# Twenty output products put off to the end of a graph-attention layer, and their bias as one bf16 product

## The chip, the cores and the metric

The kernel runs on one core of a Trainium2 chip. The metric is the device time of one execution in microseconds, as the median of several runs. The profile is one execution, in which every instruction of TensorE (PE), VectorE (DVE), ScalarE (ACT), GpSimd (POOL) and the DMA queues is recorded with its start and duration.

## The reference

Sixteen batches of 1024 nodes with 512 features pass through eight-head attention over one graph that all batches share, an output projection, a residual addition and a layer norm without scale:

```python
q = (x @ Wq + bq).reshape(b, n, H, HD)          # b = 16, n = 1024, H = 8, HD = 64, all float32
k = (x @ Wk + bk).reshape(b, n, H, HD)
v = (x @ Wv + bv).reshape(b, n, H, HD)
scores = jnp.einsum('bqhd,bkhd->bhqk', q, k) / jnp.sqrt(jnp.float32(HD))
scores = scores + (1.0 - adj)[None, None, :, :] * -1000000000.0
attn = jax.nn.softmax(scores, axis=-1)
out = jnp.einsum('bhqk,bkhd->bqhd', attn, v).reshape(b, n, d)
y = out @ Wo + bo
return _layernorm(x + y, axis=-1)
```

The graph is sparse: a node has few neighbours, and the number varies from node to node.

## The kernel before

**Tiles and blocks.** The nodes are ranked by their number of neighbours once, and each batch is worked in eight tiles of 128 ranked nodes. The attention of a tile is a list of blocks: for block i, every one of the 128 nodes takes its i-th neighbour, whose key and value row is gathered from DRAM by an indirect DMA on POOL (`gather`, line 961, 128 rows of 4 KB into `kvg`). VectorE multiplies queries with keys (`products`, line 982) and sums by head (`scores`, line 986); ScalarE takes the exponentials (line 996) and weighs the values (line 1006), VectorE adds them up (line 1022). The few nodes with more neighbours get extra blocks, which TensorE adds with a selection matrix (`sum`, lines 1031 and 1032). A batch has 34 blocks, all batches together 544.

**Front products.** Ahead of the attention of a batch come its transposes of x (`pxT`), its query products (`pq`, line 619) and key and value products, done as a seven-product scheme of block combinations (`x`, `pp`, `z`, line 743, with the elementwise combinations on VectorE). They run about two batches ahead and go to DRAM as `q_rows` and `kv_rows`.

**Output.** `normalise` and `turn` divide by the sum of the weights and transpose the result (`poT`), and ScalarE copies it to `oT`. `finish` then issues four products with Wo (`po`, line 619) for the tile, adds residual and bias, and normalises: line 844 adds the residual and line 845 the bias with the row sum, ScalarE squares and applies the norm (lines 852 and 866), and POOL scatters the rows to the output (line 870). Once the front products are over and blocks are left, the bias is added by TensorE instead: a fifth f32 product of a column of ones with the bias (line 917, `biased`), so that VectorE has one operation per tile there, not two.

**Put off.** Ten tiles, numbers 102 to 111 of 128, are not finished in turn. Their `oT` goes to DRAM (`spill`), and after the front products it is brought back (`reload`, line 815, into the free tiles e, w and g) together with the residual. For tiles from 102 on the residual is kept in DRAM in ranked order as well (`residual`, stored at line 593 when x has been transposed, loaded at line 809), so that it comes back by a plain DMA on SyncE and not by a gather on POOL (line 797).

**Order.** The order of all instructions is fixed when the program is built. A loop runs over steps n from -39 to the end; step n does the early parts of blocks n+4, n+3 and so on and the last part of block n, and then hands TensorE work from two lists, `finishing` before `fronts`, as long as a credit lasts. The credit grows in each step by a share, which in the middle is what the front products and the output products of a batch need:

```python
share = (max(0.0, left - goal) + NT * NPAIR * PRODUCT + NS * SUM) / NBT
```

From batch 13 on the share spreads the rest of the front products up to step 498; after that it is `LAST_SHARE`. Each engine and each DMA queue takes its instructions strictly in this order. Work meant for a later step is put in by `later` (in the same step ahead of the block's last part) and `later_last`.

Of the kernel before, what the change touches and what calls it, by code (L numbers as in the profile page):

```python
# [10 lines left out]
F32 = mybir.dt.float32  # L11
BF16 = mybir.dt.bfloat16
I32 = mybir.dt.int32
AF = mybir.ActivationFunctionType
OP = mybir.AluOpType
# [16 lines left out]
KG_BUFS, Q_BUFS, QT_BUFS, PV_BUFS, Y_BUFS = 8, 5, 3, 5, 6  # L32
# [3 lines left out]

LAZY = 2

SPILL = range(102, 112)

AHEAD_LAST = 11

# [1 line left out]
EARLY = 13  # L44

FIRST = 11
# [9 lines left out]
PRODUCT = 0.86  # L56
SUM = 0.87
TRANSPOSE = 0.44
LEAD_SHARE = 3.3
START_SHARE = 2.0  # L60
LAST_SHARE = 3.0

P = 128

# [102 lines left out]
def kernel(  # L167
# [36 lines left out]
    nc = tc.nc  # L204
    B, N, D = x.shape
    HD = D // HEADS
    NPAIR = D // P
# [35 lines left out]
    with ExitStack() as main:  # L243
# [24 lines left out]
        before = one.tile([P, P], F32, name="before")  # L268
        bq_bc = one.tile([P, D], F32, name="bq_bc")
        bk_norm = one.tile([P, 1], F32, name="bk_norm")  # L270

        B11, B21, B22, T1, T2, T3, T4 = (
            work.tile([P, 2, D], F32, tag=name, name=name, bufs=1) for name in ("b11", "b21", "b22", "t1", "t2", "t3", "t4")
# [24 lines left out]
        order_views = dram_disjoint_views(order, NT)  # L298
        out_views = dram_disjoint_views(out, B * NT)
        x_rows = x.rearrange("b n d -> (b n) d")  # L300
        spill = [dram.tile([P, D], F32, name=f"spill_{i}") for i in range(len(SPILL))]
        residual = [dram.tile([P, D], F32, name=f"residual_{i}") for i in range(B * NT - SPILL[0])]
        zeros = work.tile([P, D + HEADS], F32, tag="pv0", name="zeros", bufs=3)
        nc.gpsimd.memset(zeros, 0.0)
        bias_rows = work.tile([2 * NPAIR, D + HEADS], F32, tag="pv0", name="bias_rows", bufs=3)[:, 0:P]
# [58 lines left out]
            nc.vector.tensor_tensor(bo_bc, pb, bo_bc, op=OP.add)  # L364

        now, plan, rest, urgent, known, waiting, combined = [0], {}, {}, [], [], [], []

        def later(k, fn):  # L370
            plan.setdefault(now[0] + k, []).append(fn)
# [209 lines left out]
        def transpose_x(b, t):  # L581
            def pe():
                xs = X.pop((b, t))
                p = fill_psum(f"pxT_{b}_{t}")
                for c in range(NPAIR):
                    nc.tensor.transpose(p[:, ts(c, P)], xs[:, ts(c, P)], ident)  # L586

                def out():
                    XT[b, t] = work.tile([P, D], F32, tag="xT", name=f"xT_{b}_{t}", bufs=4)
                    nc.scalar.copy(XT[b, t], p)  # L590
                    n = b * NT + t + 3
                    if b * NT + t >= SPILL[0]:
                        nc.sync.dma_start(residual[b * NT + t - SPILL[0]], xs)
                        later(2, lambda: load_x(n // NT, n % NT))
                    else:
                        load_x(n // NT, n % NT)
                    if t % 2 and (b, t) != (0, 1):
                        later(1, combine)

                def combine():  # L600
                    s = [work.tile([P, HD2], F32, tag=f"s{i}", name=f"s{i}_{b}_{t}", bufs=1 + i // 4) for i in (1, 2, 3, 4)]
                    x0, x1 = XT[b, t - 1], XT[b, t]
                    nc.vector.tensor_tensor(s[0], x1[:, 0:HD2], x1[:, HD2:D], op=OP.add)
                    nc.vector.tensor_tensor(s[2], x0[:, 0:HD2], x1[:, 0:HD2], op=OP.subtract)
                    nc.vector.tensor_tensor(s[1], s[0], x0[:, 0:HD2], op=OP.subtract)  # L605
                    nc.vector.tensor_tensor(s[3], x0[:, HD2:D], s[1], op=OP.subtract)
                    SX[b, t // 2] = s

                later(1, out)

            return [(TRANSPOSE, pe, lambda: (b, t) in X)]
# [179 lines left out]
            units += unit("z", s(4), B22, False, out_v0, "v1")  # L791
            return units

        loaded, half = {}, []

        def gather_x(y, b, t):
            nc.gpsimd.indirect_dma_start(  # L797
# [4 lines left out]
        def load_y(b, t, k=None):  # L802
            if k is None:
                Y[b, t] = work.tile([P, D], F32, tag="y", name=f"y_{b}_{t}", bufs=Y_BUFS)
            else:
                Y[b, t] = work.tile([P, 2, D], F32, tag=f"t{k % 4 + 1}", name=f"y_{b}_{t}", bufs=1)[:, 0, :]
            loaded[b, t] = now[0]
            if b * NT + t >= SPILL[0]:
                nc.sync.dma_start(Y[b, t], residual[b * NT + t - SPILL[0]])
            else:  # L810
                gather_x(Y[b, t], b, t)

        def reload(b, t, k):
            OT[b, t] = work.tile([P, D], F32, tag="ewg"[k % 3], name=f"oTs_{b}_{t}", bufs=1)
            nc.sync.dma_start(OT[b, t], spill[b * NT + t - SPILL[0]])
            load_y(b, t, k)
            later(2, lambda: done.append((b, t)))

        def finish(b, t):
# [9 lines left out]
            def out(p):  # L829
# [4 lines left out]
                if single:  # L834
                    st = small.tile([P, 5], F32, name="stats", bufs=6)
                else:

                    second = bool(half)
                    if not second:
                        half.append([small.tile([P, 2, 5], F32, name="stats_2", bufs=3)])  # L840
                    st2 = half[0][0]
                    st = st2[:, int(second), :]
                if fronts_then:
# [71 lines left out]
            if biased:  # L915
                def bias():
                    nc.tensor.matmul(
                        PS[f"po_{b}_{t}"], ident[:, 0:1].to_broadcast([P, P]), bo_bc, start=False, stop=False
                    )

                units.insert(2, (PRODUCT, bias, None))
            return units


# [136 lines left out]
        def turn(b, t, o):  # L1061
            def transpose():
                p = fill_psum(f"poT_{b}_{t}")
                for c in range(NPAIR):
                    nc.tensor.transpose(p[:, ts(c, P)], o[:, ts(c, P)], ident)  # L1065

                def out():
                    OT[b, t] = work.tile([P, D], F32, tag="oT", name=f"oT_{b}_{t}", bufs=LAZY + 2)
                    nc.scalar.copy(OT[b, t], p)
                    if b * NT + t in SPILL:  # L1070
                        later(1, lambda: nc.sync.dma_start(spill[b * NT + t - SPILL[0]], OT.pop((b, t))))
                        spilled.append((b, t))
                    else:
                        later(1, lambda: done.append((b, t)))

                later(1, out)

            later(1, lambda: urgent.append(transpose))
            if not fronts:
                coming.append((b, t))  # L1080
# [71 lines left out]
        prep.setdefault(CHECKS_AT, []).append(checks())  # L1152
        preps = [loads(), ranks()]
        prep.setdefault((B - 1) * NBT, []).append(guard())
        with tc.manual_schedule():

            fronts += transpose_x(0, 0) + transpose_x(0, 1)
# [11 lines left out]
            while n < total or plan or rest or urgent or done or finishing or spilled or not guarded:  # L1169
                now[0] = n  # L1170
                if n < 0:
                    share = START_SHARE if n > FRONT_BY else LEAD_SHARE if n > -LEAD_IN else TRANSPOSE * 1.5
                elif n >= SPILL[0] // NT * NBT + NBT:

                    share = sum(u[0] for u in fronts) / max(fronts_end - n, 1) + NS * SUM / NBT if fronts else LAST_SHARE
                elif n % NBT == 0:

                    left = sum(u[0] for u in fronts)
                    ahead = EARLY + FIRST * (1 - max(0, n // NBT - 1) / (SPILL[0] // NT))
                    goal = fronts_time - (n // NBT + 2 + ahead / NBT) * batch_time  # L1180
                    share = (max(0.0, left - goal) + NT * NPAIR * PRODUCT + NS * SUM) / NBT
                if 0 <= n + 3 < total:
                    exponentials(n + 3)
                if 0 <= n + 4 < total:
# [25 lines left out]
                    if tile_done not in loaded and sum(b * NT + t not in SPILL for b, t in Y) < 5:  # L1210
                        load_y(*tile_done)
                coming[:] = [t for t in coming if t not in loaded]
                if spilled and not fronts and n > last_reload + 2 and sum(b * NT + t in SPILL for b, t in Y) < 3:
                    reload(*spilled.pop(0), reloads)
                    reloads, last_reload = reloads + 1, n
                first_unit = True
                while credit > 0 or urgent:
                    if urgent and not (first_unit and fronts):
                        urgent.pop(0)()
                        continue  # L1220
                    if (
                        not finishing and len(done) > (LAZY if fronts else 0) and n > loaded.get(done[0], n) + 1
                        and n > last_finish + 1 and not total - 2 <= n < total
                    ):
                        finishing = finish(*done.pop(0))
                        last_finish = n
                    units = finishing or fronts
                    if not units:
                        if urgent:
                            urgent.pop(0)()  # L1230
                            continue
                        break
                    cost, fn, ready = units[0]
                    if ready and not ready():
                        if urgent:
                            urgent.pop(0)()
                            continue
                        break
                    del units[0]
                    fn()  # L1240
                    credit -= cost
                    first_unit = False
# [40 lines left out]
```

## Time and profile before

| | us |
|---|---|
| median of 3 runs | 1944.96 |
| lowest and highest | 1942.09, 1947.64 |
| the profiled execution's own time | 1947.77 |
| its span, first to last instruction | 1946.0 |

The profile counts busy time as the union of an engine's instructions. An f32 product is two instructions (the output products are 1024 instructions), and successive ones overlap, so the mean duration of a row is longer than what one costs in a series; the distance between starts is that. "DMA share" is the mean busy share of the core's 16 DMA engines.

### The profile page before, as it was taken

What the parts mean: (1) busy time and instruction counts of PE and PEld (TensorE: products, weight loads), DVE (VectorE), ACT (ScalarE), POOL (GpSimd) and SP (SyncE); (2) the same over time, 40 slices, a digit from 0 to 9 for tenths busy, and PEclk for the clock granted to TensorE, in tenths of its full rate; (3) what the DMA queues carried; (4) which work ended last, traced back from release to release, by engine and by line L of the source; (5) the groups of instructions that cost most, each with busy time, mean ns of one, the idle gap of its engine ahead of it and who ended that gap; (6) DMA issues with size and microseconds to landing.
All of it is one profiled execution on the core that took longest, in us unless ns stands there. A gap on an engine that the chain in (4) does not pass through costs nothing.

```text
span 1946.0 us, 25024 instructions
## 1 busy us (share of the span) xinstructions
PE 1872.7 (96%) x5259; PEld 905.5 (47%) x5259; DVE 1730.4 (89%) x3496; ACT 1550.5 (80%) x6072; POOL 1380.3 (71%) x1283
## 2 busy tenths in 40 slices
PE   8989999899999999999999999999999999889896
PEld 3434454444544454444545445454544444344443
DVE  6888889899998999989999989999998998989894
ACT  3638779778888888888888878888888798879694
POOL 1336667878787677877887777777777777766684
PEclk9999999999999999999999999999999999999998
DMA  7357788888889788887888888888888989998994
GB/s 271 121 177 244 249 275 271 289 271 285 290 276 315 252 296 274 272 309 256 300 280 301 275 279 304 288 296 269 296 295 291 317 284 350 320 328 267 349 302 146
DMA packets 183104, 541.40 MB, mean 278 GB/s; under 512 B 30783, under 2 KB 30795, under 8 KB 182942
## 3 DMA queue, kind: packets, MB, share of 16 engines
q0 software_dynamic: 134864, 451.79, 69.5%
q1 hardware_dynamic: 45184, 82.41, 11.8%
q10 hardware_dynamic: 2894, 5.52, 0.9%
q8 instruction: 44, 0.72, 0.1%
q14 instruction: 118, 0.97, 0.1%
HBM read 423.93 MB, written 140.37 MB: 290 GB/s over the span
## 4 chain that ended last, share of the span: by engine, by line
PE 73%; DVE 10%; DMA 5%; issue 3%; ACT 2%; POOL 1%; SPq 0%; POOLq 0%; DVEq 0%; ACTq 0%
PE po L619 18%; PE pq L619 16%; PE pp L743 13%; PE z L743 9%; PE x L743 9%; DMA kvg<-kv_rows,key_row 2%; DVE qk L982 2%; PE poT L1065 2%; PE pxT L586 2%; DVE s L986 2%; PE sum L1032 2%; PE sum L1031 1%; ACT pv L1006 1%; DVE pv L1022 1%; PE pm L688 1%
## 5 line engine op out<-in xcount | busy, mean ns | idle before, releaser
L1006 ACT ACTIVATE pv<-kvg,pv 128x64 f32<-128x64 f32 x3544 | 892.6, 339 | 0.0
L961 POOL DMA_INDIRECT kvg<-kv_rows,key_row x544 | 621.3, 1142 | 233.2 <-issue 85.9
L619 PE MATMUL po<-wo,oT 128*128 128x512 f32 x944 | 437.4, 596 | 2.0 <-DVE y L844 1.1
L619 PE MATMUL pq<-wq,xT 128*128 128x512 f32 x904 | 425.9, 600 | 0.9 <-DVE g L762 0.7
L986 DVE TENSOR_REDUCE s<-qk 128x8 f32<-128x512 f32 x544 | 369.8, 680 | 8.1 <-ACT y L866 0.5
L982 DVE TENSOR_TENSOR qk<-qt,kvg 128x512 f32<-128x512 f32 x448 | 306.2, 683 | 35.8 <-DMA kvg<-kv_rows,key_row 29.9
L619 PEld LDWEIGHTS po<-wo,oT 128*128 128x128 f32 x944 | 176.9, 191 | 199.2 <-issue 185.5
L619 PEld LDWEIGHTS pq<-wq,xT 128*128 128x128 f32 x904 | 169.2, 192 | 196.3 <-issue 179.0
L743 PE MATMUL pp<-t,s 128*128 128x512 f32 x504 | 237.1, 593 | 0.5 <-DVE s L605 0.5
L743 PE MATMUL x<-b,xT 128*128 128x512 f32 x504 | 237.0, 592 | 0.0
L1022 DVE TENSOR_TENSOR pv<-pv,pv 128x520 f32<-128x520 f32 x336 | 232.9, 693 | 1.5 <-ACT pv L1006 1.5
L996 ACT ACTIVATE pv<-s,absent 128x8 f32<-128x8 f32 x448 | 130.4, 294 | 81.5 <-DVE s L986 75.4
L797 POOL DMA_INDIRECT x<-in_x_dram,asked_row x120 | 133.7, 1114 | 76.7 <-PE pxT L586 46.1
L870 POOL DMA_INDIRECT out_dram<-y,asked_row x128 | 144.9, 1132 | 36.5 <-issue 21.4
L665 POOL DMA_INDIRECT kv_rows<-kv,asked_row x120 | 138.9, 1158 | 35.1 <-issue 20.9
L629 ACT ACTIVATE sq_k<-kv 128x128 f32<-128x128 f32 x512 | 150.9, 300 | 6.3 <-DVE kv L766 6.3
L743 PEld LDWEIGHTS x<-b,xT 128*128 128x128 f32 x504 | 94.7, 190 | 113.6 <-issue 109.2
L743 PEld LDWEIGHTS pp<-t,s 128*128 128x128 f32 x504 | 94.5, 190 | 110.7 <-issue 101.6
L931 POOL DMA_INDIRECT qg<-q_rows,query_row x96 | 108.1, 1126 | 34.2 <-issue 23.8
L797 POOL DMA_INDIRECT y<-in_x_dram,asked_row x102 | 108.8, 1066 | 32.3 <-issue 30.2
L743 PE MATMUL z<-b,s 128*128 128x512 f32 x252 | 120.7, 602 | 5.1 <-DVE kv L771 4.9
L743 PE MATMUL z<-t,s 128*128 128x512 f32 x252 | 120.6, 601 | 0.0
(200 smaller groups left out, 2666.8 us busy)
## 6 DMA issues: line engine op xcount, KB each, us to landing
q_rows<-q SPq DMA_DIRECT2D x113, 256.0 KB
qt<-q_rows SPq DMA_DIRECT2D x105, 256.0 KB
kvg<-kv_rows,key_row POOLq DMA_INDIRECT x544, 5.8
residual<-x SPq DMA_DIRECT2D x26, 256.0 KB
y<-residual SPq DMA_DIRECT2D x26, 256.0 KB
adj<-in_adj_dram POOLq DMA_DIRECT2D x8, 512.0 KB, 12.7
kv_rows<-kv SPq DMA_DIRECT2D x8, 512.0 KB
spill<-oT SPq DMA_DIRECT2D x10, 256.0 KB
```

The source lines that it names most:

```text
L619: nc.tensor.matmul(p, lhs(c), w[:, c, :], start=(c == 0), stop=(c == NPAIR - 1))
L629: nc.scalar.activation(sq, s[:, ts(h, P)], AF.Square, scale=scale, accum_out=sums[:, h:h + 1])
L665: later(2, lambda: nc.gpsimd.indirect_dma_start(out=kv_views[b % ROWS][tt[i]], out_offset=bass.IndirectOffsetOnAxis(ap=asked_row[:, tt[i]: ...
L743: nc.tensor.matmul(R[bank], l[:, ts(c, P)], right[:, c, :], start=(first and c == 0), stop=(c == 1), skip_group_check=True,)
L797: nc.gpsimd.indirect_dma_start(out=y, out_offset=None, in_=x_rows, in_offset=bass.IndirectOffsetOnAxis(ap=asked_row[:, t:t + 1], axis=0), ...
L870: nc.gpsimd.indirect_dma_start(out=out_rows[b, t], out_offset=bass.IndirectOffsetOnAxis(ap=asked_row[:, t:t + 1], axis=0), in_=y, in_offse ...
L961: nc.gpsimd.indirect_dma_start(out=KG[n], out_offset=None, in_=kv_rows[b % ROWS], in_offset=bass.IndirectOffsetOnAxis(ap=key_row[:, g:g + ...
L982: nc.vector.tensor_tensor(QK[n], q, KG[n][:, 0:D], op=OP.mult)
L986: nc.vector.tensor_reduce(S[n], QK.pop(n).rearrange("p (h d) -> p h d", d=HD), axis=AX.X, op=OP.add)
L996: nc.scalar.activation(PV[n][:, D:], S.pop(n), AF.Exp, bias=bias)
L1006: nc.scalar.activation(pv[:, ts(h, HD)], v[:, ds(D + h * HD, HD)], AF.Copy, scale=pv[:, D + h:D + h + 1])
L1022: nc.vector.tensor_tensor(PV[b, t], PV[b, t], pv, op=OP.add)
```

## The change

The tiles put off become twenty: every fourth tile from number 36 to 96 (the first and fifth tile of a batch, from the fifth tile of batch 4 to the first of batch 12), and 102 to 105. Tiles 106 to 111 are finished in turn again. The residual is stored in DRAM for all of these and for all tiles from 102 on. The share of a batch counts only the output products that stay in it, and the reference point of the schedule's lead (`LATE`) stays at batch 12. After the front products a reload comes in every second step instead of every third, up to seven reloaded residuals may be held instead of three (two to a double tile, of seven tile names instead of four), and a tile may be finished in every step instead of every second.

The bias product of these tiles is one bf16 product: `bias_pieces` splits the bias once into three bf16 values, the rounded bias, the rounded rest and the rest of the rest, in rows 0, 32 and 64 of `bo_3`, and `three` is a column with ones in those rows.

```diff
-SPILL = range(102, 112)
+SPILL = (*range(36, 100, 4), *range(102, 106))
+STORED = {*SPILL, *range(102, 128)}
+LATE = 12
...
-LAST_SHARE = 3.0
+LAST_SHARE = 3.4
+BIAS = 0.22
...
+        def bias_pieces():
+
+            r = work.tile([P, D], F32, tag="y", name="bo_rest", bufs=Y_BUFS)
+            nc.vector.tensor_copy(bo_3, bo_bc)
+            nc.vector.tensor_tensor(r, bo_bc, bo_3, op=OP.subtract)
+            yield
+            nc.vector.tensor_copy(bo_3[32:33, :], r[32:33, :])
+            nc.vector.tensor_copy(bo_3[64:65, :], r[64:65, :])
+            nc.vector.tensor_tensor(r[64:65, :], r[64:65, :], bo_3[64:65, :], op=OP.subtract)
+            nc.vector.tensor_copy(bo_3[64:65, :], r[64:65, :])
+            yield
+            st = small.tile([P, 1], F32, name="two", bufs=1)
+            nc.vector.tensor_tensor(st, ident[:, 0:1], ident[:, 32:33], op=OP.add)
+            nc.vector.tensor_tensor(three, st, ident[:, 64:65], op=OP.add)
...
-                    if b * NT + t >= SPILL[0]:
-                        nc.sync.dma_start(residual[b * NT + t - SPILL[0]], xs)
+                    if b * NT + t in STORED:
+                        nc.sync.dma_start(residual[b * NT + t], xs)
                         later(2, lambda: load_x(n // NT, n % NT))
...
-                Y[b, t] = work.tile([P, 2, D], F32, tag=f"t{k % 4 + 1}", name=f"y_{b}_{t}", bufs=1)[:, 0, :]
+                if k % 2 == 0:
+                    tag = ("t1", "t2", "t3", "t4", "b11", "b21", "b22")[k // 2 % 7]
+                    wide.append(work.tile([P, 2, D], F32, tag=tag, name=f"y_{b}_{t}", bufs=1))
+                Y[b, t] = wide[-1][:, k % 2, :]
...
-                        half.append([small.tile([P, 2, 5], F32, name="stats_2", bufs=3)])
+                        half.append([small.tile([P, 2, 5], F32, name="stats_2", bufs=5)])
...
-                        PS[f"po_{b}_{t}"], ident[:, 0:1].to_broadcast([P, P]), bo_bc, start=False, stop=False
+                        PS[f"po_{b}_{t}"], three.to_broadcast([P, P]), bo_3, start=False, stop=False
...
-                units.insert(2, (PRODUCT, bias, None))
+                units.insert(2, (BIAS, bias, None))
...
+        prep.setdefault(NBT, []).append(bias_pieces())
...
-                elif n >= SPILL[0] // NT * NBT + NBT:
+                elif n >= (LATE + 1) * NBT:
...
-                    share = (max(0.0, left - goal) + NT * NPAIR * PRODUCT + NS * SUM) / NBT
+                    kept = sum(i not in SPILL for i in range(n // NBT * NT, n // NBT * NT + NT))
+                    share = (max(0.0, left - goal) + kept * NPAIR * PRODUCT + NS * SUM) / NBT
...
-                if spilled and not fronts and n > last_reload + 2 and sum(b * NT + t in SPILL for b, t in Y) < 3:
+                if spilled and not fronts and n > last_reload + 1 and sum(b * NT + t in SPILL for b, t in Y) < 7:
...
-                        and n > last_finish + 1 and not total - 2 <= n < total
+                        and n > last_finish + bool(fronts) and not total - 2 <= n < total
```

More of the change, by code (lines that the diff above doesn't have):

```diff
@@ L270 @@
         bk_norm = one.tile([P, 1], F32, name="bk_norm")
+        bo_3 = one.tile([P, D], BF16, name="bo_3")
+        three = one.tile([P, 1], BF16, name="three")
         B11, B21, B22, T1, T2, T3, T4 = (
@@ L300 @@
         x_rows = x.rearrange("b n d -> (b n) d")
-        spill = [dram.tile([P, D], F32, name=f"spill_{i}") for i in range(len(SPILL))]
-        residual = [dram.tile([P, D], F32, name=f"residual_{i}") for i in range(B * NT - SPILL[0])]
+        spill = {i: dram.tile([P, D], F32, name=f"spill_{i}") for i in SPILL}
+        residual = {i: dram.tile([P, D], F32, name=f"residual_{i}") for i in sorted(STORED)}
         zeros = work.tile([P, D + HEADS], F32, tag="pv0", name="zeros", bufs=3)
@@ L792, in pair @@
             return units
-        loaded, half = {}, []
+        loaded, half, wide = {}, [], []
         def gather_x(y, b, t):
@@ L805, in load_y @@
             else:
-                Y[b, t] = work.tile([P, 2, D], F32, tag=f"t{k % 4 + 1}", name=f"y_{b}_{t}", bufs=1)[:, 0, :]
+                if k % 2 == 0:
+                    tag = ("t1", "t2", "t3", "t4", "b11", "b21", "b22")[k // 2 % 7]
+                    wide.append(work.tile([P, 2, D], F32, tag=tag, name=f"y_{b}_{t}", bufs=1))
+                Y[b, t] = wide[-1][:, k % 2, :]
             loaded[b, t] = now[0]
-            if b * NT + t >= SPILL[0]:
-                nc.sync.dma_start(Y[b, t], residual[b * NT + t - SPILL[0]])
+            if b * NT + t in STORED:
+                nc.sync.dma_start(Y[b, t], residual[b * NT + t])
             else:
@@ L814, in reload @@
             OT[b, t] = work.tile([P, D], F32, tag="ewg"[k % 3], name=f"oTs_{b}_{t}", bufs=1)
-            nc.sync.dma_start(OT[b, t], spill[b * NT + t - SPILL[0]])
+            nc.sync.dma_start(OT[b, t], spill[b * NT + t])
             load_y(b, t, k)
@@ L1070, in out @@
                     if b * NT + t in SPILL:
-                        later(1, lambda: nc.sync.dma_start(spill[b * NT + t - SPILL[0]], OT.pop((b, t))))
+                        later(1, lambda: nc.sync.dma_start(spill[b * NT + t], OT.pop((b, t))))
                         spilled.append((b, t))
@@ L1178 @@
                     left = sum(u[0] for u in fronts)
-                    ahead = EARLY + FIRST * (1 - max(0, n // NBT - 1) / (SPILL[0] // NT))
+                    ahead = EARLY + FIRST * (1 - max(0, n // NBT - 1) / LATE)
                     goal = fronts_time - (n // NBT + 2 + ahead / NBT) * batch_time
-                    share = (max(0.0, left - goal) + NT * NPAIR * PRODUCT + NS * SUM) / NBT
+                    kept = sum(i not in SPILL for i in range(n // NBT * NT, n // NBT * NT + NT))
+                    share = (max(0.0, left - goal) + kept * NPAIR * PRODUCT + NS * SUM) / NBT
                 if 0 <= n + 3 < total:
```

## The prediction

> **What bounds the kernel now.** I read the page first (busy shares, the 40 slices, the chain), then the groups, then the busy time by stage, and last the waits and the timeline of the tail.
>
> ```profile
> PE 1872.7 (96%) x5259; PEld 905.5 (47%) x5259; DVE 1730.4 (89%) x3496; ACT 1550.5 (80%) x6072; POOL 1380.3 (71%) x1283
> ...
> PE   8989999899999999999999999999999999889896
> ...
> DMA  7357788888889788887888888888888989998994
> ...
> PE 73%; DVE 10%; DMA 5%; issue 3%; ACT 2%; POOL 1%; SPq 0%; POOLq 0%; DVEq 0%; ACTq 0%
> ```
>
> TensorE carries 73% of the chain and is at nine tenths in nearly every slice until the last seven. There its digit falls to 8 and 6 while DMA rises to 9. So there are stages with different limits, and the change moves work from one to another. A step of the schedule multiplies block n+4 by its keys, so the times of line 982 on VectorE date the steps: step 136 (batch 4) is at 612.5, 442 (batch 13) at 1630.0, 474 at 1722.4, 498 (the front products end) at 1795.6, 538 at 1908.0. Busy time by stage:
>
> ```profile
> core 0: us, PE busy (x) PEld busy (x) DVE busy (x) ACT busy (x) POOL busy (x), PEclk, DMA share, GB/s
> 612.50:1630.00 1017.50, 1005.95 (x2860) 488.68 (x2859) 933.70 (x1852) 855.58 (x3398) 780.91 (x726) 1.00 0.86 289
> 1630.00:1722.40 92.40, 81.96 (x236) 39.67 (x234) 86.40 (x159) 81.94 (x349) 67.76 (x58) 0.98 0.95 333
> 1722.40:1795.60 73.20, 69.68 (x188) 34.02 (x189) 69.75 (x136) 62.38 (x249) 43.91 (x40) 0.95 0.82 282
> 1795.60:1908.00 112.40, 103.26 (x273) 47.85 (x272) 99.00 (x236) 92.97 (x336) 85.24 (x77) 0.97 0.92 322
> 1908.00:1946.00 38.00, 21.52 (x59) 10.83 (x57) 13.46 (x47) 11.94 (x25) 13.10 (x13) 0.85 0.29 104
> 320.60:386.80 66.20, 60.10 (x177) 30.76 (x176) 56.56 (x114) 56.41 (x230) 53.57 (x49) 0.98 0.86 285
> ```
>
> In batches 4 to 12 TensorE is busy 99% and VectorE 92%. Busy overlaps in a pipelined engine, so I price TensorE by starts. The timeline:
>
> ```profile
> 1784.45 3.60 PE L619 MATMUL po<-wo,oT 128*128 128x512 f32 x8
> 1787.88 1.88 PE L743 MATMUL pp<-t,s 128*128 128x512 f32 x4
> ...
> 1801.22 1.02 PE L917 MATMUL po<-bo_bc,ident 128*128 128x512 f32 x2
> 1802.07 1.88 PE L619 MATMUL po<-wo,oT 128*128 128x512 f32 x4
> ```
>
> Four f32 products take 1787.88 - 1784.45 = 3.43 us, 0.858 each; a bias product is two such instructions, 0.85. Multiplied with the instructions as built, steps 136 to 441 hold 999.6 us of TensorE work in 1017.5 us of time: TensorE is the limit there, with 2% lost. Steps 442 to 497 hold 144.4 in 165.6, and 498 to the end 115.1 in 150.4: the tail has TensorE time to spare, 21 and 35 us.
>
> **The change part by part.** All counts are from the two built orders.
>
> *Batches 4 to 12.* Sixteen tiles leave: output products fall from 284 to 220, 64 x 0.858 = 54.9 us. The smaller share also lets eight front products and eight transposes slip past step 441, 7.8 us. TensorE work: 999.6 to 936.9. At the old 2% loss that gives 954 us. VectorE loses for each tile these two (busy, mean ns of one, then idle before), and two small ones:
>
> ```profile
> L845 DVE SCALAR_TENSOR_TENSOR y<-bo_bc,y 128x512 f32<-128x512 f32 x105 | 72.8, 694 | 3.6
> L844 DVE TENSOR_TENSOR y<-po,y 128x512 f32<-128x512 f32 x105 | 71.7, 683 | 11.7 <-PE po L619 11.7
> ```
>
> and one of the waits (total us, times, longest) is
>
> ```profile
> DVE qk L982 <- DMA kvg<-kv_rows,key_row: 33.6, 27, 4.3
> ```
>
> Back to back in the chain, such an operation costs 0.61, so a tile is about 0.61 + 0.69 + 2 x 0.15 = 1.6 us, 16 of them 25.6: VectorE 933.7 to 908. VectorE cannot be full: at 1630 to 1722.4, where ten tiles were put off already and TensorE had room, it was busy 86.40 / 92.40 = 0.935. At that share 908 takes 971 us. So TensorE's limit is 954, VectorE's 971. Part of VectorE's idle time today is waiting for TensorE (11.7 us in the row above), which shrinks, and what is late next is the key gather (33.6 us over the span). I take 966, a gain of 51; ends -64 and, at the share of the last window above (56.56 / 66.20 = 0.854, so 1063 us), +46, which is where the slower rival comes from.
>
> *Batches 13 and 14 to the end of the front products.* Tiles 106 to 111 are finished in place: 24 more output products (20.6 us) plus the slipped front work, 144.4 to 172.7. The share formula of this stretch does not count output products, so the fronts crowd into the last steps: 34.8 us of TensorE work in steps 490 to 497 against 28.8. Steps 442 to 473 were VectorE's (92.4 us) and get 5 more of its work: 97. Steps 474 to 497 hold 88.5 us of TensorE work against 70.5 in 73.2: at 0.98, 90. Together 187 against 165.6: +22 (ends +16, +28).
>
> *The tail.* Output products go from 92 to 132 (+34.4 us). The bias: 22 f32 products, 18.9 us, become 32 bf16 ones. No row shows a bf16 product. The nearest is the f32 one: two instructions of 0.43. One bf16 instruction can cost from 0.21 (half of one f32 instruction) to 0.43; the Trainium skill, "TensorE: Matmul & The Clock Gate", section "Back-to-back issue gap", gives 215.7 ns for 512 columns, and an exact half of the row agrees, so I take 0.22, 7 us; at 0.43 it is 7 more. TensorE work 115.1 to 137.4, of it in steps 498 to 537 from 98.1 to 121.8. That part took 112.4; 121.8 at a share of 0.95 is 128: +16. Ten more reloads, ten more residual loads and ten more stores are 30 x 0.262 = 7.9 MB on top of 322 GB/s x 112.4 us = 36.2 MB. Here a rule speaks against the change: the skill's "DMA: Bandwidth & Descriptors", section "Specifications", puts a core's HBM limit at about 358 GB/s, which makes 44.1 MB an estimate of 123 us. By the row, 322 at a share of 0.92 is 350 at full, 126 us, and 1820 to 1840 moved 392, 112 us. I use 126, so DMA and TensorE come to about the same, and two equal limits cost a little: +17 (ends +10, +30). The end after 1908, a chain of one last tile, keeps its 38.
>
> *The clock.* The same TensorE page, Part 1, says an idle window of about 3.4 us halves the clock for one; here the granted clock is 1.00 in the full middle, and 0.98 and 0.95 in the two looser rows after it, 0.86 between 1722.4 and 1746.1. The rule speaks against loosening the middle. By the row, 0.98 of 966 would cost 19 us if TensorE were critical at each dip; as the dips come where it idles, I count three of them at 1.7, 5 us, inside my 966. By the rule alone, with every stall a dip, the gain of 51 would be 32.
>
> *Costed at nothing.* The split of the bias (six operations of 512 columns and two small ones, 4 us of VectorE in batch 1) lies beside TensorE, which has no idle time from 274.6 to 350: +1, 4 without that cover. SyncE gets 27 more stores in the middle (16 spills, 11 residuals; 7.1 MB on 289 x 1.0175 = 294, while 16 gathers of 0.262 leave POOL, so +1% net); they queue behind q stores on which SyncE waits anyway. The store that now reads x lets the gather of x three tiles on start two steps later on POOL; a pair of transposes comes every eight steps, which hides it. If not, key gathers behind it on POOL wait about 2 us each time, 27 times at most. The larger limits on buffers (seven residuals, five statistics) and a finish in every step instead of every second only permit; what they let in is priced in the tail.
>
> **Sum.** -51 + 1 + 22 + 17 = -11. The profiled execution took 1947.77 (span 1946.0); it becomes 1936.8. Its time is 2.8 above the median of the runs, 1944.96, so I predict 1934.
>
> **The rivals.** *TensorE limits throughout (-30).* The middle at 954 and a tail that packs: -64 + 1 + 20 + 13 = -30, 1915. For it: 222.8 us of batches 9 and 10 with TensorE never idle; VectorE held 44.91 of 45.50 us at 1630 to 1675.5. Against: both engines then need over 95%.
>
> *The middle becomes VectorE's and the gathers' (slower).* The mechanism: with TensorE lighter, each late key gather stops the multiply on line 982, and everything behind it on VectorE, and no TensorE backlog covers that. The price: VectorE at a share of 0.91 makes the middle 998, a gain of 19 against 40 given back: +21, 1966. It decides at 908 / (1017.5 - 40) = 0.929; above, the change gains. For it: 320.6 to 386.8, with a TensorE load as light as the new one, ran no faster than the rest (3.31 us per step). Against: 0.935 at 1630 to 1722.4 with DMA at 0.95.
>
> *Reloads come late.* A reload stands two steps before its product instead of three, in SyncE's queue behind residual loads that wait for a store to land. A load of the same size took 5.27 us to land in the tail's chain, and two steps are 5.6. Eight of twenty reloads 2.5 us late stop TensorE for 20: +9, 1954. Against: SyncE runs ahead, and the leads before were 9.5 us and more.
>
> *The bf16 product is no cheaper:* at 0.86, 32 cost 20.5 more than planned, again 1954; I give it no chance of its own.
>
> **How the numbers follow.** No change is anything within 0.3%, 5.8 us, about what a measurement of this kernel can tell. My forecast gets 0.50 (0.39 faster, 0.11 within), TensorE throughout 0.25 (faster), the slow middle 0.14 (0.12 slower, 0.02 within), late reloads 0.11 (0.06 slower, 0.03 within, 0.02 faster): 0.66, 0.16, 0.18. The range, 1910 to 1956, takes in the fast rival and late reloads and leaves out most of the slow middle; the likeliest case's own is 1924 to 1944.
>
> **What would show it.** Right: batches 4 to 12 in about 966 us with VectorE near 0.94; the bias product as one instruction of about 0.22 between starts; steps 442 to 497 near 187; TensorE busy over 95% from 498 on; no wait of a po product for a reload. Wrong: the middle above 978, rows of line 982 waiting for kvg well over 34 us, or TensorE idle for oTs in the tail.

## The result: faster by 0.75%, and where it came from

The changed kernel takes 1930.15 us (median) against 1943.22 for the kernel before, measured together; the ratio is 0.9925 with a 95% interval of 0.9907 to 0.9944. The profiled execution has a span of 1926.8 us against 1946.0. One of the changed kernel's six executions took 2801.22 us at a granted clock of 0.654; it counts in the median and not in the ratio.

The experiments further down ran later: `c1` and `e1` to `e8` on what the record calls chip 0, `e10` to `e13` on its chip 9 (for the first comparison no chip is on record). On both the kernel before took 2007 us, 3% more. In the changed kernel's profile on chip 0 most of the extra time lies in isolated long steps, eleven of 7.2 to 12.8 us in steps 136 to 441 where the first profile has three. The experiments are therefore compared with kernels of their own chip, and mostly by stages.

The page of the changed kernel, its busy times and the slices:

```profile
PE 1854.1 (96%) x5247; PEld 898.2 (47%) x5247; DVE 1724.8 (90%) x3494; ACT 1549.6 (80%) x6072; POOL 1368.9 (71%) x1262
...
PE   7989999999999999999999999999999989899996
...
DMA  7357788888889898898989898988899898888994
...
PE 10%; issue 1%; DVE 1%; POOL 1%; DMA 1%; ACT 0%; POOLq 0%; SPq 0%; DVEq 0%
```

The shares have hardly moved: TensorE is at 96% before and after, of a shorter span. What moved is where it is idle: the four slices before the last (1686 to 1879 us) are now all at 9, where before three of the last six had fallen to 8, and the one 8 that is left close to them (slice 35, 1638 to 1686 us) holds a stall that is looked at below. The chain in the last line could be followed back through a small part of the span only (its shares sum to 14%), so it is not compared. The stages tell the story. These are the same steps as in the five rows of before (136 to 441, 442 to 473, 474 to 497, 498 to 537, the end); columns as there:

```profile
core 0: us, PE busy (x) PEld busy (x) DVE busy (x) ACT busy (x) POOL busy (x), PEclk, DMA share, GB/s
610.80:1578.80 968.00, 949.39 (x2728) 463.34 (x2726) 905.77 (x1767) 833.12 (x3359) 747.81 (x678) 1.00 0.89 303
1578.80:1679.70 100.90, 84.95 (x232) 40.74 (x233) 90.48 (x177) 81.75 (x329) 71.61 (x64) 0.96 0.87 301
1679.70:1763.40 83.70, 83.70 (x234) 40.28 (x233) 76.03 (x152) 68.72 (x271) 50.88 (x49) 0.99 0.84 283
1763.40:1892.10 128.70, 128.07 (x357) 60.15 (x355) 107.90 (x275) 107.81 (x375) 95.97 (x88) 1.00 0.95 342
1892.10:1926.80 34.70, 18.24 (x51) 9.47 (x51) 13.58 (x50) 12.68 (x27) 14.39 (x16) 0.85 0.24 95
```

| steps | before | predicted | after | difference |
|---|---|---|---|---|
| up to 135 | 612.5 | 613.5 | 610.8 | -1.7 |
| 136 to 441 | 1017.5 | 966 | 968.0 | -49.5 |
| 442 to 473 | 92.4 | 97 | 100.9 | +8.5 |
| 474 to 497 | 73.2 | 90 | 83.7 | +10.5 |
| 498 to 537 | 112.4 | 128 | 128.7 | +16.3 |
| 538 to the end | 38.0 | 38 | 34.7 | -3.3 |

In the middle both engines are now close to full: TensorE 949.39 / 968.00 = 0.98, VectorE 905.77 / 968.00 = 0.936. In the tail TensorE is busy 128.07 of 128.70 us, where before it was busy 103.26 of 112.40. The differences sum to -19.2 us, that of the two spans. The medians lie only 13.1 us apart: the profiled execution of the kernel before, 1947.77 us, was slower than its median, 1943.22.

### The profile page after: what moved, and what is told of

The parts are those of the page before. It is cut to its first block, busy times and chain, and to the rows that moved or that the text cites. A ratio compares the mean times of both kernels' runs of the same rounds, so it can differ in the third digit from the quotient of the medians.

```text
span 1926.8 us, 25037 instructions
## 1 busy us (share of the span) xinstructions
PE 1854.1 (96%) x5247; PEld 898.2 (47%) x5247; DVE 1724.8 (90%) x3494; ACT 1549.6 (80%) x6072; POOL 1368.9 (71%) x1262
## 5 line engine op out<-in xcount | busy, mean ns | idle before, releaser
L639 PE MATMUL po<-wo,oT 128*128 128x512 f32 x864 | 401.2, 597 | 1.0 <-ACT oT L1092 0.9
L639 PEld LDWEIGHTS po<-wo,oT 128*128 128x128 f32 x864 | 162.9, 191 | 182.9 <-issue 169.4
L763 PE MATMUL pp<-t,xT 128*128 128x512 f32 x252 | 118.4, 592 | 0.0
```

The lines of the kernel that those rows point to most:

```text
L639: nc.tensor.matmul(p, lhs(c), w[:, c, :], start=(c == 0), stop=(c == NPAIR - 1))
L763: nc.tensor.matmul(R[bank], l[:, ts(c, P)], right[:, c, :], start=(first and c == 0), stop=(c == 1), skip_group_check=True,)
```

## The experiments

### Either half alone

Two kernels take the change apart. `e1_bias_only` is the kernel before with the new bias product:

```diff
-                        PS[f"po_{b}_{t}"], ident[:, 0:1].to_broadcast([P, P]), bo_bc, start=False, stop=False
+                        PS[f"po_{b}_{t}"], three.to_broadcast([P, P]), bo_3, start=False, stop=False
...
-                units.insert(2, (PRODUCT, bias, None))
+                units.insert(2, (BIAS, bias, None))
```

> The kernel before with the bias product alone made bf16 (22 products, same tiles put off). Theory, TensorE has room in the tail of the kernel before (115.1 us of work in 150.4): the 22 x 0.64 = 14 us are mostly idle time made longer, the run gains 2 to 5 us (1938 to 1941 against 1943). Rival, TensorE already limits that tail: it gains 12 to 14 us, all of what the whole change gains (1930).

Measured: ratio 1.0005 (0.9979 to 1.0031). In its profile steps 498 to 537 take 112.3 us, as in the kernel before (112.4, in the first comparison), although TensorE is busy 11 us less in them (92.07 against 103.26). That tail had TensorE time to spare; cheaper products there buy nothing. Of the 2 to 5 us that were expected, up to 4 lie within the interval, and so does no gain at all.

`e2_f32_bias` is the changed kernel with the first of these two edits taken back (the bias product is again an f32 one), its order of instructions untouched.

> The changed kernel with its 32 bias products done in f32 as before, same order of instructions. It adds 32 x 0.64 = 20.5 us of TensorE work after step 498. Theory, TensorE limits the tail once twenty tiles are put off: steps 498 to 537 go from 128.7 to about 147, the run from 1930 to 1949, slower than before. Rival, the transfers limit that tail (0.95 DMA share): less than 6 us are lost.

Measured: ratio 1.0026 (0.9997 to 1.0056), no faster than before. Steps 498 to 537 took 148.5 us, 19.8 more than in the changed kernel's first profile and 16.4 more than in its profile on the same chip. So putting off twenty tiles with f32 bias products gives back in the tail what the middle gains, and the two halves of the change pay only together.

`c1_changed_again` is the changed kernel on chip 0.

> The changed kernel unaltered, as the measure for the other kernels of its chip. Every theory: 0.992 of the kernel before. Theory, the gain of the middle stands on how prompt the gathers are: on a chip where they land late it is smaller, and the ratio nearer to 1.

Measured: ratio 0.996 (0.9918 to 1.0002). The interval holds the expected 0.992 and also no change, so on this chip the time of the whole execution does not show the gain by itself; the medians of all executions, 1994.10 and 2007.14, stand at 0.9935. The stages show it. They are listed in us, also for the kernels that the next sections introduce; `e3`, `e4` and `e12` leave work out and ran once each:

| | 136 to 441 | 442 to 473 | 474 to 497 | 498 to 537 | end |
|---|---|---|---|---|---|
| e1_bias_only (tiles as before) | 1071.0 | 90.5 | 73.3 | 112.3 | 37.7 |
| c1_changed_again | 1023.8 | 101.8 | 84.1 | 132.1 | 34.7 |
| e2_f32_bias | 1022.8 | 102.3 | 83.9 | 148.5 | 38.4 |
| e4_no_reloads | 1014.1 | 100.4 | 84.4 | 138.0 | 36.4 |
| e3_half_products | 991.2 | 100.8 | 83.9 | 134.0 | 35.7 |
| e5_even_share | 1008.1 | 100.4 | 77.6 | 126.7 | 34.4 |
| e11_even_again | 1023.0 | 100.6 | 77.6 | 128.3 | 33.0 |
| e6_sixteen | 1035.9 | 108.0 | 77.3 | 130.3 | 30.1 |
| e8_bias_everywhere | 1009.1 | 104.6 | 79.7 | 126.7 | 34.7 |
| e13_bias_again | 1017.1 | 107.2 | 78.9 | 128.3 | 34.7 |
| e10_last_share | 1025.5 | 102.2 | 77.6 | 121.4 | 35.8 |
| e12_both | 979.0 | 105.5 | 78.9 | 126.7 | 34.4 |

Here too the middle is 47 us shorter than with the tiles as before, so the stages do not bear out that the gain is smaller where gathers are late. Nor do the gathers hold VectorE up longer there: its multiply waits for them 11.0 us in the middle of c1, and 28.5 us in that of the first comparison. One profile settles no small difference: kernels with the same middle differ by 10 us in this column on one chip (c1 and e4) and by 15 us between the two (e5 and e11).

### What limits the tail: TensorE or the transfers

`e4_no_reloads` leaves out the transfers that bring the put-off tiles and their residuals back:

```diff
-            if b * NT + t in STORED:
+            if k is not None:
+                nc.gpsimd.memset(Y[b, t], 1.0)
+            elif b * NT + t in STORED:
...
-            OT[b, t] = work.tile([P, D], F32, tag="ewg"[k % 3], name=f"oTs_{b}_{t}", bufs=1)
-            nc.sync.dma_start(OT[b, t], spill[b * NT + t])
+            OT[b, t] = W["o"][:, 0, :]
```

> The changed kernel without the DMAs that bring the twenty tiles back in the tail: the products take a slice of Wo in place of the reloaded tile, and the residual is a constant set by POOL (20 memsets, about 0.5 us each). 40 transfers of 0.262 MB less after step 498, TensorE work unchanged. Theory, TensorE limits the tail: steps 498 to 537 stay at 125 to 129 us. Rival, transfers or late reloads limit it: 110 to 118.

The whole stretch took 138.0 us, outside both ranges and 5.9 more than in c1: 2.5 of it lie in steps 498 to 505, 3.4 in steps 526 to 537, and their cause is open. Steps 506 to 525, between these and chosen after the result, agree. Busy time of these steps in c1, in e4 and in e2 (f32 bias), in this order, all on chip 0:

```profile
1862.70:1931.50 68.80, 68.59 (x190) 32.75 (x193) 56.37 (x157) 54.98 (x182) 51.13 (x46) 1.00 0.93 339
```
```profile
1850.30:1919.00 68.70, 68.49 (x189) 32.73 (x192) 56.07 (x155) 54.88 (x182) 53.60 (x52) 1.00 0.68 220
```
```profile
1864.80:1944.80 80.00, 80.00 (x212) 37.79 (x211) 56.54 (x157) 56.35 (x185) 48.58 (x47) 1.00 0.83 284
```

Without the reloads the DMA share falls from 0.93 to 0.68 and the time stays (68.8 and 68.7 us): transfers and reload order cost nothing in these steps. With f32 bias they take 11.2 us longer; 17 bias products stand in them, and each is dearer by 0.64 us (0.86 against 0.22), 17 x 0.64 = 10.9. TensorE's added work goes into these steps one for one.

### What limits the middle

`e3_half_products` takes away TensorE work alone. It leaves out the second and third of a tile's four output products:

```diff
             units = product(f"po_{b}_{t}", lambda c: OT[b, t][:, ts(c, P)], W["o"], out)
+            if 4 * NBT <= now[0] < 13 * NBT:
+                units[1:3] = [(PRODUCT, lambda: None, None)] * 2
```

> The changed kernel with the second and third of the four output products of every tile left out in steps 136 to 441 (their place in the order and their cost in the credit stay): 110 products, 94 us of TensorE work less there, nothing changed on the other engines. It shows how close the next limit is. Theory, VectorE and its gathers follow close behind: steps 136 to 441 take 940 to 955 us instead of 968. Rival one, TensorE is still the only limit: 870 to 880. Rival two, VectorE limits already: 963 to 970.

`e8_bias_everywhere` takes VectorE work away: TensorE adds the bias from batch 2 on. It rests on e5 below, counts BIAS in the share and has

```diff
-            biased = not fronts and now[0] < total
+            fronts_then = bool(fronts) and now[0] < 2 * NBT
+            biased = not fronts_then and now[0] < total
...
-            fronts_then = bool(fronts)
```

> As e5, with the bias by the bf16 product from batch 2 on, so VectorE has one operation less for 80 tiles (about 0.61 each) and TensorE 0.22 more. In steps 136 to 441 TensorE work is 947 instead of 936.9, VectorE loses 34 us. Theory, TensorE is still the first limit of the middle: it takes 3 to 10 us longer. Rival, VectorE has become the limit: it takes 15 to 30 us less.

`e13_bias_again` is e8 once more, on chip 9.

> The kernel e8_bias_everywhere once more, beside e11. Theory, VectorE and TensorE limit the middle together, so 34 us off the one and 10 us onto the other cancel: within 0.3% of e11. Rival, one of them limits: over 0.5% apart, slower if it is TensorE.

`e12_both`, on chip 9, is e8 with the edit of e3.

> e8 with the second and third output product of every tile left out in steps 136 to 441, as in e3: about 94 us of TensorE work and 34 us of VectorE work less than in the changed kernel. Alone, the first took about 30 us off the middle and the second nothing. Theory, the two limits lie within a few per cent of each other and only both together give way: the middle 955 to 975 us where e5 and e8 took 1008. Rival, the gathers are the third limit right behind them: 985 to 1000, no better than e3's 991.

Steps 136 to 441 of c1, e3, e8 and e12, in this order (the last two windows begin and end 0.8 us late, which leaves their length as it is):

```profile
624.30:1648.10 1023.80, 967.94 (x2730) 469.54 (x2730) 905.22 (x1767) 835.85 (x3351) 741.58 (x676) 0.98 0.85 285
```
```profile
615.30:1606.50 991.20, 891.25 (x2504) 428.84 (x2502) 904.67 (x1767) 836.52 (x3367) 748.21 (x676) 0.97 0.87 295
```
```profile
623.50:1632.60 1009.10, 964.80 (x2723) 470.60 (x2759) 872.14 (x1711) 826.81 (x3332) 737.83 (x677) 0.98 0.86 290
```
```profile
625.00:1604.00 979.00, 899.64 (x2529) 437.94 (x2563) 866.59 (x1711) 831.32 (x3359) 742.87 (x677) 0.96 0.88 299
```

94 us of TensorE work less bring 33 against c1 (23 against e4, which has the same middle): more than if VectorE alone were the limit, far less than if TensorE were. The clock takes part of it back. By the trace's clock records it stood at 0.50 for 64.9 us of e3's stage, with TensorE busy in 54.2 of them; in c1 it was 47.8 and 34.8. At half the clock half of such busy time is lost, an estimate of 27 us in e3 against 17 in c1.

34 us of VectorE work less, with 10 more on TensorE, bring nothing that can be seen: e8 has 1009.1 and e13 1017.1, the same kernel without it (e5 and e11) 1008.1 and 1023.0, and the ratios are 0.9861 (0.9811 to 0.9911) and 0.9884 (0.984 to 0.9928) against 0.9875 (0.983 to 0.9919) and 0.99 (0.9856 to 0.9944). The 15 to 30 us less of e8's rival did not come. Whether TensorE's 3 to 10 us more did cannot be told from these profiles. The ratio of e13 is within 0.3% of e11's, as expected, but the intervals are too wide to exclude the 0.5% of its rival.

Both taken together give 979.0, between what the theory (955 to 975) and its rival (985 to 1000) expected, and no further from e3's 991.2 than two profiles can differ. TensorE is then busy 0.92 and VectorE 0.89 of the stage, and neither is full. The gathers alone do not explain this: of VectorE's 112 us of idle time 21.0 end at a key gather (12 times, 5.1 at most), and its longest waits, 6.8 to 7.7 us, end at operations of the front products. The clock stood at 0.50 for 75.1 us, with TensorE busy in 55.7 of them, an estimate of 28 us lost. What holds this middle was not tested by itself and stays open.

### The stall at step 471, and a better version

Steps 442 to 473 took 100.9 us where 97 were predicted. One row of VectorE's timeline of the changed kernel explains it, with POOL's rows of the same moment (in brackets the idle time before, and what ended it):

```profile
1675.88 0.69 DVE L1005 TENSOR_TENSOR qk<-qt,kvg 128x512 f32<-128x512 f32 x1 [9.24 <-DMA kvg<-kv_rows,key_row]
```
```profile
1662.78 1.50 POOL L685 DMA_INDIRECT kv_rows<-kv,asked_row  x1 [0.30 <-issue]
1668.80 1.03 POOL L984 DMA_INDIRECT kvg<-kv_rows,key_row  x1 [4.51 <-DMA kv_rows<-mean]
```

VectorE stands for 9.24 us at the first gather of batch 14 (step 471 took 11.2 us, 11.5 in c1). POOL could not issue it, since the last keys and values of that batch and their mean row had only just been written: its front products had been crowded out. (The releaser in brackets is the landing of the mean row.) From batch 13 on the share does not count the output products of tiles that are finished in turn. Before, there were none until batch 14; now there are six. `e5_even_share` counts them:

```diff
                 elif n >= (LATE + 1) * NBT:
 
-                    share = sum(u[0] for u in fronts) / max(fronts_end - n, 1) + NS * SUM / NBT if fronts else LAST_SHARE
+                    kept = sum(i not in SPILL for i in range((LATE + 1) * NT, (LATE + 2) * NT))
+                    share = (
+                        sum(u[0] for u in fronts) / max(fronts_end - n, 1) + (kept * NPAIR * PRODUCT + NS * SUM) / NBT
+                        if fronts else LAST_SHARE
+                    )
```

> The changed kernel with the output products of batch 13 on counted in the share until the front products end, so that front work is spread over steps 442 to 497 (97.1 and 75.6 us of TensorE work before and after step 474 instead of 84.2 and 88.5). Theory, the crowding of front work before step 498 costs time: steps 442 to 497 take 177 to 179 us instead of 184.5, the run gains 6. Rival, VectorE limits these steps whatever the spread (its work there is the same): under 2 us.

> The kernel e5_even_share once more, as the measure for the others of this call. Every theory: 0.985 to 0.99 of the kernel before, steps 442 to 497 in 177 to 179 us.

`e11_even_again` is e5 on chip 9. Steps 442 to 497 take 178.0 and 178.2 us against 185.9 in c1, and no step of 442 to 473 is longer than 5.8 us: the long wait is gone with the crowding. The ratio to the kernel before is 0.9875 (0.983 to 0.9919) on chip 0, where c1 has 0.996 (0.9918 to 1.0002), and 0.99 (0.9856 to 0.9944) on chip 9.

`e6_sixteen` then moves tiles 102 to 105 back (`SPILL = tuple(range(36, 100, 4))` on top of e5).

> As e5, with sixteen tiles put off, 102 to 105 finished in turn. TensorE work after step 498 falls from 137.4 to 121 us, before it rises by 16. Theory, TensorE limits the tail and has room at 442 to 497 once the share is even: the tail loses 14 us, the stage before it gains no more than 8 over e5, the run is 8 to 12 us faster than the changed kernel. Rival, the tail is held by transfers or the order of reloads: no faster than e5.

Measured: ratio 0.9947 (0.9921 to 0.9973), slower than e5, and with a median of 1996.19 us no faster than c1 (1994.10). So the expected 8 to 12 us did not come. The stage 442 to 497 grew by 7 us as expected, and the end shrank by 4, but steps 498 to 537 took 130.3 us against 126.7. TensorE was busy only 115 us of them; its profile has a stall of 8 us there (ScalarE before a copy of `oT`) whose cause the trace does not name. Whether the tail would be shorter without it is open. The profiles also overstate the difference: that of e6 is the slowest of its 15 executions, that of e5 the fastest of its 6.

`e10_last_share` is e5 with `LAST_SHARE = 2.8`.

> e5 with LAST_SHARE 2.8 instead of 3.4: TensorE work in steps 498 to 537 falls from 121.8 to 116.2 us, that after step 538 rises from 15.6 to 21.0, where TensorE is idle half of the time. Theory, the tail is TensorE's and the end is a chain of one tile that leaves room: 4 to 6 us off the one, 0 to 3 onto the other, the run 2 to 5 us faster than e11. Rival, the products left over stand in front of the last tile's and lengthen its chain one for one: no difference.

Measured: ratio 0.9867 (0.9827 to 0.9908), beside e11 with 0.99 (0.9856 to 0.9944). The totals do not separate them, nor these two from e5, e8 and e13. In the stages, one profile each, steps 498 to 537 go from 128.3 to 121.4 us, the end from 33.0 to 35.8, 4 us in all, as the theory had it. From step 442 to the end e10 takes 337.0 us, the least of the kernels that put off twenty tiles, against 352.7 in c1.

## Why the prediction was right, point by point

**The middle, 966 predicted, 968.0 measured.** The step that decided was to take VectorE's limit from the one stage where TensorE already had room. Its share there was 0.935, and in the new middle it is 905.77 / 968.00 = 0.936. TensorE's own limit of 954 was not reached. But that VectorE is the limit at this share is not shown. On chip 0 the same kernel's middle has a share of 905.22 / 1023.80 = 0.88, and 34 us of VectorE work less (e8) brought nothing that can be seen. The middle lies where TensorE and VectorE both come near to full; that the two shares agree to a thousandth is in part luck. The wait that was to come next did grow; the multiply's waits for gathers in the middle, before and after (us in total, times, longest), and over the whole execution after:

```profile
DVE qk L982 <- DMA kvg<-kv_rows,key_row: 17.7, 18, 4.3
```
```profile
DVE qk L1005 <- DMA kvg<-kv_rows,key_row: 28.5, 21, 4.5
```
```profile
DVE qk L1005 <- DMA kvg<-kv_rows,key_row: 51.9, 31, 9.2
```

The last line is one of the prediction's own signs of being wrong (waits "well over 34 us"; it was 33.6), and it came. Of the 18.3 us more, 10.8 lie in the middle and 5.8 in steps 442 to 473, with the one wait of 9.2 us at step 471. The middle stayed under 978 all the same, because VectorE's other waits shrank: its idle time there fell from 83.8 to 62.2 us in all.

**Steps 442 to 497, +22 predicted, +19 measured.** The sum was close, its parts less so. The first part was put 4 us too low: the text saw that fronts would crowd into the last steps, but priced that as TensorE work alone and missed the stall of 9.24 us in which the gathers of batch 14 wait for crowded-out fronts. The second part was put 6 us too high: TensorE was busy all of its 83.7 us and must have finished the 88.5 us of work in the next stage, which the sums by stage do not allow for. That the two errors nearly cancel is luck.

**The bias, 0.22 predicted.** The timeline of the changed kernel:

```profile
1803.73 0.38 PE L940 MATMUL po<-bo,three 128*128 128x512 bf16 x1
1803.95 1.02 PE L639 MATMUL po<-wo,oTs 128*128 128x512 f32 x2
```

1803.95 - 1803.73 = 0.22 us between starts, one instruction. In all 32 the distance is 0.215 or 0.216 us, as the 215.7 ns have it that the prediction took (the Trainium skill's "TensorE: Matmul & The Clock Gate" has them in its section "Wait — 56ns, not 53.3ns?"). The rival of a bf16 product that is no cheaper is out.

**The tail, +17 predicted.** Steps 498 to 537 came out at 128.7 us for 128, by TensorE as the text had it. Its second reason was wrong: the transfers were put at 126 us, as a limit of the same size, with 350 GB/s as full. The stretch moved 342 GB/s at a share of 0.95, but in the kernel without reloads steps 506 to 525 are no faster. What the tail had to spare was TensorE's, and it was used up. The end took 3.3 us less than the 38 that were kept for it; c1 has the same 34.7, and the reason is open.

**The clock.** The prediction put 5 us into its 966 for three dips of the granted clock, and 19 if every stall were one. In the new middle there was one, of 3.4 us, and the row shows 1.00. On chip 0 it weighs more: the clock is 0.98 there, and the same products keep TensorE busy for 967.94 us instead of 949.39.

**The sum.** The spans differ by 19.2 us, where -11 was predicted: the middle was 1.5 worse, steps 442 to 497 3.0 better, the tail 0.7, the start 2.7 and the end 3.3 better. The last two were put at +1 and 0 and are not explained.

**Costed at nothing.** The split of the bias in batch 1 left it at 112.5 us (112.2 before). The residual stores that POOL's gathers of x now wait for ended 9.8 us of POOL's idle time in all, 3 times where 27 at most were allowed for. One of the three reached VectorE: POOL waited 2.98 us until 1562.54, the key gather behind it was issued at 1565.26 and landed at 1571.37, and the multiply waited 2.82 us for it.

**The rivals.** The slow middle was to decide at a VectorE share of 0.929; 0.936 was measured, so it was near. Late reloads: taking the reloads away did not shorten steps 506 to 525, and neither the weight loads that read the reloaded tiles (`oTs`) nor their products waited for a transfer, as their groups of the changed kernel show (busy us, mean ns | idle us just before, and what ended it):

```profile
L639 PEld LDWEIGHTS po<-wo,oTs 128*128 128x128 f32 x160 | 29.9, 190 | 30.0 <-issue 28.4 <-DVE stats L878 0.5 <-DVE pv L1045 0.2
L639 PE MATMUL po<-wo,oTs 128*128 128x512 f32 x160 | 74.9, 592 | 0.0
```

TensorE throughout: no; the middle did not reach 954, and on chip 0 e3 shows that TensorE's work alone does not set it.

## What to carry to other kernels

When work is moved from a stage that one engine limits to a stage where that engine has room, ask what the first stage will meet next. A stage of the same kernel in which the first engine is already relieved gave a good estimate here (2 us off), although the experiments do not show that the second engine is then the limit. The room in the receiving stage is finite: here it took the cheaper bias to make it, and for either half alone no gain was measured. A pacing rule that leaves the moved work out of its sum shows up as a single long wait somewhere else (here one of 9 us), so look for the longest wait of a stage, not only for its shares.

## What the runs showed of the hardware that was not expected

With the DMA engines at a share of 0.93 and 339 GB/s, steps 506 to 525 of the tail ran at the same speed as at 0.68 and 220 GB/s: a high DMA share alone was no sign of a limit.

The same program took 3% longer on chip 0 than in the first comparison (1994.10 and 1930.15 us). In steps 136 to 441 its median step hardly differed (3.13 us against 3.08), and one multiply of VectorE took 0.684 us in both; most of the difference lay in the eleven long steps. The granted clock made them dearer. In c1's step 263 TensorE stood idle for 6.62 us; from 1059.1 to 1069.3 us the clock was 0.50, and the two instructions of a query product, elsewhere 1.02 us together, took 2.07. VectorE had waited 10.3 us there, up to 1060.0, for a releaser that the trace does not name, with the DMA engines at a share of 0.98. What starts these stalls was not tested.
